# A four-layer image kernel: mixer output and last projection merged into one centred matrix, and a gate computed as one pass of 96 output rows

## The chip, the cores and the metric

The kernel runs on one core of a Trainium2 chip. The metric is the device time of one execution in microseconds (us). Each kernel was run three times; the median is given with the lowest and the highest run.

## What is computed

The input is a batch of 8 images with 256 channels and 32 x 32 pixels, in float32. Four residual layers follow each other, `x = x + layer(group_norm(x))` with 32 groups: a softmax attention on normalised queries and keys with 8 heads of 64 channels (layer 0), a 3 x 3 convolution with scaled sign weights (layer 1), a 3 x 3 convolution (layer 2), and a mixer (layer 3). The mixer is where the change lies. Cut to what matters:

```python
xs  = tokens(group_norm(x))                  # 1024 tokens x 256 channels
xm  = mamba(layernorm(xs)) + skip * layernorm(xs)    # 4 branches of 64 channels
Q   = conv1d(conv1d(xm, qdw_w, qdw_b, groups=4, pad=1), qpw_w, qpw_b)   # 256 -> 4 -> 4
xg  = sigmoid(Q) * xm                        # one gate per branch and token
R   = conv1d(depthwise3(xg), rpw_w) + xg
xm2 = conv1d(depthwise3(concat(xs, R)), fpw_w) + xs
x_local  = depthwise3(xm2, lc_w, lc_b)
x_global = mha(xm2)                          # ... attention output o, then
                                             # o @ attn_outw.T + attn_outb
x_out = concat(x_local, x_global) @ fc_w.T + fc_b
x_out = gelu(layernorm(x_out))               # over the 256 channels of a token
xi    = depthwise_conv3x3(instance_norm(x_out))
out   = layernorm(xi) @ proj_w.T + proj_b
```

The layernorm after `fc_w` subtracts, for each token, the mean over the 256 channels, and divides by the root of the mean square of what is left. All biases of this layer's setup are zero except `m_dtb`; the kernel treats them as given.

## The kernel before

**Layout.** Channels lie on the 128 partitions, in two tiles of 128 channels, and the 1024 tokens lie along the free axis. Everything is float32. A product with 256 input and 256 output channels is 8 matmuls of 128 x 128 weights and 512 columns: two output tiles, two input tiles, two halves of the tokens. In a trace every such float32 matmul appears as two records.

**Recording and order.** Operations of TensorE, VectorE and ScalarE go through the helper class `Paced` (L91 to L112), so the profile shows nearly all of them at line L101 and they are told apart by tile names. A scheduler places the instructions of each engine; each engine then works through its own queue in order and waits at an instruction whose inputs or buffers are not there. All DMAs are issued by SP, also in order. `urgent()` (L124) gives the small operations of a statistic a higher place in the schedule.

**Pools.** Large intermediates come from a pool of 12 work tiles, matmul results from two PSUM tiles of 1024 columns (`big`), one of 512 (`acc`) and two of 512 for the scans (`da`). Streamed weights come through `chunk` (L149 to L157), from six slots.

**Images in a pipeline.** For image b, `front_attention` (L576, layer 0) and `front_convs` (L750, layers 1 and 2) come first; then `scan_layers` (L1000), the selective scans of the mixer, which use VectorE, GpSimd (POOL), ScalarE and a little of TensorE; then `back_layers` (L1151), `back_out` (L1237) and `back_end` (L1263), the rest of the mixer. The main loop runs, for each b, the scans of image b beside the dense work of other images: the back layers of image b-1 and the front of image b+1. `interleave` (L1335) does this with costs: each `yield` of the dense stream gives a cost (about the TensorE time in us), and whenever the sum of costs passes a due time the next piece of the scans is recorded and the due time grows by PACE (1.8 for the first image, 2.95 for the middle six, 1.6 for the last). What is left of the scans when the dense stream ends is recorded behind it; with the given costs nothing is left. In a middle step the dense costs add up to 459.4 and the scans' due times to 433.6. After the loop, the back layers of the last image run alone.

**The order inside a middle step.** `dense()` (L1369) runs `back_layers` of image b-1 to its end, with its mixer attention (`mixer_attention`, L1044); then four pieces of the next image's front, which are the products for the values V (`islice(front, 4)`); then the first two pieces of `back_out`, which are the product with `attn_outw` (tile name `aout`, result `glob`); then one more piece of the front, the first pair's Q and K; then the rest of `back_out`, the product of the concatenated `local` and `glob` with `fc_w`; then the front's attention; then the two convolutions of the front with `back_end` laid between.

**The places that the change touches.**

- `back_layers`, L1156 to L1172: the gate. For both token halves, two channel tiles and three taps, `qdw[:, j, k]` (128 x 4) is multiplied with the tokens shifted by one tap: 12 matmuls with 4 output rows. One ScalarE pass adds the bias and gives `q4` (4 x 1024). Four matmuls with `qpr` (4 x 128) spread it over the channels, and tanh and a multiplication follow.
- `mixer_attention`, `take` and `finish` (L1092, L1119, L1136): the attention output `o` is multiplied by the inverse of the sums and the value bias is added, one VectorE pass each. The inverse comes through `invert` (L472): a DMA to DRAM and back, a reciprocal, and a DMA that spreads it (`rs<-inv`).
- `back_out`, L1237: `project_both` (L390) with `aout`, 8 matmuls; a ScalarE pass for each half of `glob`; `project_both` with `fcw`, 16 matmuls; a ScalarE pass for each half of the result `xo`, which goes to DRAM.
- `back_end`, L1263: `xo` is loaded again; `layer_norm` (L293) multiplies it with `mean_w` (4 matmuls), subtracts (VectorE, tile names `xo<-xo,big`), squares (ScalarE, `ln_sq`), and sums the squares by matmuls into `acc`.

Beside them matter `group_stats` (L256), whose chain of small matmuls and small VectorE operations must end before a convolution can begin (`im` is its normalised input), and `scan_steps` (L885).

## Time and profile before

| | |
|---|---|
| median of 3 runs | 6621.78 us (6604.92 to 6635.64) |
| the profiled execution | 6632.25 us |
| span in its profile | 6630.4 us |
| mean granted TensorE clock | 0.892 |
| TensorE matmul busy | 5708.6 us, 86% of the span |
| VectorE, ScalarE, GpSimd busy | 59%, 41%, 40% |
| DMA queue of SP | 467.90 MB, 25.4% of 16 engines |

A group row of the profile gives line, engine, operation, output and input tile with their shapes, the count, the busy time, the mean of one in ns, and the idle time of the engine just ahead of them with what ended it. For matmuls, `128*4` means 128 rows (contraction) by 4 columns of weights (output rows). In a timeline, `[8.44 <-DVE o L101]` means that the engine stood idle for 8.44 us and that a VectorE instruction that writes `o` ended it. The windows view gives the busy time of each engine in a stretch of the span.

In the trace the gate of the eight images starts at 1007.0, 1780.7, 2562.4, 3340.5, 4118.8, 4900.6, 5668.5 and 6298.3 us. These marks divide the span: up to 1007 us the front of the first two images and the first scans; six middle stages of 768 to 782 us; a stage of 630 us with the last scans; and the last image's back layers, alone, 332 us.

### The profile page before, as it was taken

The page shows a single profiled execution, that of the slowest core. Times are in us where ns is not written, and L with a number is a line of the kernel's source. Part 1 is how long each engine was busy: PE and PEld are TensorE (multiplying, and loading weights), DVE is VectorE, ACT ScalarE, POOL GpSimd, SP SyncE. Part 2 cuts the span into 40 slices and gives each one's busy share as a digit, 9 for nine tenths or more (in the row PEclk, how much of TensorE's full clock was granted, in tenths as well). Part 3 has the DMA queues.
Part 4 walks back from the last instruction along what each step waited for, and adds up shares of the span by engine and source line. Part 5 has one row for each costly group of instructions (what it writes and reads, how often), then busy time and mean ns, then how long its engine had stood idle before and what let it go on. Part 6 is the DMA issues. An engine that isn't in the chain of part 4 may idle for free.

```text
span 6630.4 us, 52730 instructions
## 1 busy us (share of the span) xinstructions
PE 5708.6 (86%) x17602; PEld 1926.6 (29%) x17602; DVE 3903.6 (59%) x4613; ACT 2687.2 (41%) x3225; POOL 2684.8 (40%) x1295
## 2 busy tenths in 40 slices
PE   8887689897998979998899989999799988978596
PEld 2331133222422234222332223222342223311222
DVE  4248745577465775567655675557755676455522
ACT  4134424553254532544245432555235442344242
POOL 0016662634355251642526334462526426176300
PEclk9988888998998989899999989899899999867697
DMA  1022332322233122331223222241213212233200
GB/s 41 27 60 79 77 90 73 101 60 65 74 97 91 48 69 76 88 83 52 76 78 92 70 64 80 72 110 45 79 59 105 79 53 80 65 94 89 58 21 26
DMA packets 217969, 471.36 MB, mean 71 GB/s; under 512 B 60244, under 2 KB 103636, under 8 KB 215640
## 3 DMA queue, kind: packets, MB, share of 16 engines
q1 hardware_dynamic: 217688, 467.90, 25.4%
q8 instruction: 141, 2.31, 0.1%
q14 instruction: 140, 1.15, 0.1%
HBM read 395.36 MB, written 63.96 MB: 69 GB/s over the span
## 4 chain that ended last, share of the span: by engine, by line
PE 53%; DVE 25%; DMA 6%; issue 6%; ACT 5%; POOL 4%; SPq 1%; POOLq 0%; DVEq 0%; ACTq 0%
PE big L101 34%; PE acc L101 12%; DVE hs L101 5%; PE da L101 4%; DVE p L101 3%; PE y L101 2%; DVE u L101 2%; DVE dw L101 2%; POOL hs L963 2%; POOL hs L931 2%; DVE t L101 1%; DVE dt L101 1%; DMA du_m<-a 1%; DVE st L101 1%; ACT p L101 1%
## 5 line engine op out<-in xcount | busy, mean ns | idle before, releaser
L931 POOL TENSOR_TENSOR hs<-du,bc 128x1024 f32<-128x1024 f32 x512 | 1319.8, 2594 | 1912.6 <-DMA du<-du_m 767.4
L963 POOL TENSOR_TENSOR hs<-hs,bc 128x1024 f32<-128x1024 f32 x512 | 1278.8, 2498 | 693.2 <-DVE hs L101 480.4
L101 ACT ACTIVATE p<-big 128x1024 f32<-128x1024 f32 x1024 | 1036.1, 1019 | 769.3 <-PE big L101 764.8
L101 PE MATMUL acc<-p,v 128*64 128x512 f32 x4096 | 1189.7, 653 | 2.6 <-ACT o L101 2.6
L101 PE MATMUL big<-im,w 128*128 128x512 f32 x2304 | 1073.7, 622 | 120.9 <-ACT im L101 102.6
L101 ACT ACTIVATE da<-dt,a_neg 128x512 f32<-128x512 f32 x1024 | 688.7, 687 | 791.3 <-DVE hs L101 484.3
L101 DVE TENSOR_TENSOR p<-p 128x1024 f32<-128x1024 f32 x448 | 717.0, 1600 | 273.7 <-ACT p L101 183.9
L101 DVE TENSOR_TENSOR_SCAN hs<-da,carry,hs 128x512 f32<-128x512 f32 x512 | 628.2, 1268 | 382.8 <-POOL hs L931 301.2
L101 DVE TENSOR_TENSOR_SCAN hs<-da,hs 128x512 f32<-128x512 f32 x512 | 600.0, 1207 | 256.8 <-ACT da L101 166.3
L101 PE MATMUL big<-q,k 64*128 64x512 f32 x2048 | 602.5, 657 | 76.7 <-ACT p L101 47.8
L101 PE MATMUL big<-qk,qk 32*128 32x512 f32 x2048 | 658.2, 687 | 9.2 <-ACT p L101 6.5
L101 PEld LDWEIGHTS big<-im,w 128*128 128x128 f32 x2304 | 445.4, 198 | 752.0 <-issue 613.8
L101 PE MATMUL y<-hs,sel 128*32 128x512 f32 x2048 | 410.9, 676 | 210.9 <-POOL hs L963 180.8
L962 POOL COPY carry<-hs 128x2 f32<-128x2 f32 x256 | 97.5, 381 | 947.6 <-DVE hs L101 928.2
L101 PEld LDWEIGHTS acc<-p,v 128*64 128x64 f32 x4096 | 217.6, 140 | 843.2 <-issue 759.8
L101 PEld LDWEIGHTS big<-qk,qk 32*128 32x128 f32 x2048 | 173.8, 195 | 487.2 <-issue 269.2
L101 PEld LDWEIGHTS big<-q,k 64*128 64x128 f32 x2048 | 161.2, 188 | 503.0 <-issue 247.4
L101 PE MATMUL big<-o,w 128*128 128x512 f32 x384 | 196.2, 664 | 92.6 <-DVE o L101 92.6
L101 PE MATMUL big<-xn,w 128*128 128x512 f32 x512 | 232.4, 608 | 5.6 <-ACT p L101 5.6
L101 DVE SCALAR_TENSOR_TENSOR dw<-xo,vec,dw 128x961 f32<-128x961 f32 (+1 forms) x128 | 194.1, 1550 | 29.3 <-ACT dw L101 29.1
L101 DVE SCALAR_TENSOR_TENSOR u<-raw,vec,u 128x1024 f32<-128x1024 f32 x96 | 153.9, 1603 | 87.2 <-ACT u L101 86.7
L101 DVE SCALAR_TENSOR_TENSOR xt<-big,vec,xt 128x1024 f32<-128x1024 f32 x48 | 61.4, 1279 | 236.2 <-PE big L101 236.2
(191 smaller groups left out, 5231.1 us busy)
## 6 DMA issues: line engine op xcount, KB each, us to landing
bc<-bc SPq DMA_DIRECT2D x1024, 128.0 KB
dt<-dt_m SPq DMA_DIRECT2D x512, 128.0 KB
du<-du_m SPq DMA_DIRECT2D x512, 128.0 KB
w<-in_wc SPq DMA_DIRECT2D x192, 192.0 KB
rs<-inv SPq DMA_DIRECT2D x64, 256.0 KB
dt_m<-dt SPq DMA_DIRECT2D x64, 256.0 KB
du_m<-a SPq DMA_DIRECT2D x64, 256.0 KB
xt<-in_x SPq DMA_DIRECT2D x8, 1024.0 KB
```

Source lines behind the costliest of these rows:

```text
L101: made = issue(*args, **kwargs)
L931: nc.gpsimd.tensor_mul(u["hs"], u["du"], both_groups(u["bc"][:, 0]))
L962: nc.gpsimd.tensor_copy(carry[:, u["q"], g : g + 2], hs[:, :, HALF - 1])
L963: nc.gpsimd.tensor_mul(hs, hs, both_groups(u["bc"][:, 1]))
```

## The change

1. **Once, near the start of the program** (`merge_weights`): `attn_outw` is multiplied on TensorE with the half of `fc_w` that takes the attention output, and the biases are carried through, so that one matrix maps `o` to `x_out`. From every column of the resulting 512 x 256 matrix, and from its bias, the mean over the 256 outputs is subtracted, so that `x_out` has mean zero over the channels by construction. The matrix is stored to DRAM (`fc_w`) and streamed from there like the other weights. This stream of instructions is placed behind the ninth piece of the first image's `front_attention`.
2. **`back_out`**: the product with `aout` and the passes that make `glob` are gone; `fcw` takes `local` and `o`. In `dense()`, the Q and K of the next image's first pair now come ahead of the whole of `back_out`.
3. **`mixer_attention`**: the value bias is no longer added to `o` (it is in the merged bias).
4. **`layer_norm`** has a switch `centred`; with it the mean matmuls and the subtraction are left out. It is used for the first layer norm of `back_end`.
5. **The gate**: one product of all three taps at once: the weights of tap k stand in columns 32k to 32k+3 of 96, so 4 matmuls give 96 rows. Three ScalarE passes of 32 rows copy them with a shift of one token to the right, none, and one to the left; the two tokens at the ends are set to zero. The following matmuls contract over 96 rows instead of 4. The cost given to the planner here is 4 instead of 10.

With both, the dense costs of a middle step add up to 446.6 instead of 459.4 (of the step of the last scans 240.5 instead of 253.4); the scans' due times are as before.

The core of the diff:

```diff
@@ chunk
-        src = I[name]
+        src = fc_w if name == "fcw" else I[name]
@@ setup
-    qpw = wp.tile([NB, NB], F32, name="qpw")
-    nc.sync.dma_start(out=qpw, in_=I["qpw"])
+    qpw = wp.tile([96, NB], F32, name="qpw")
+    nc.gpsimd.memset(qpw, 0.0)
+    for k in range(3):
+        nc.sync.dma_start(out=qpw[k * 32 : k * 32 + NB], in_=I["qpw"])
...
-    qdw = wp.tile([P, 2, 3, NB], F32, name="qdw")
+    qdw = wp.tile([P, 2, 3, 32], F32, name="qdw")
@@ layer_norm
         for tok, psum in parts:
+            if centred:
+                for t in range(2):
+                    scalar.activation(sq[t][:, tok], ts[t][:, tok], AF.Square)
+                continue
@@ mixer_attention
-                    def finish(r):
-                        vector.tensor_mul(ot, ot, r)
-                        vector.tensor_scalar_add(ot, ot, col("ain_b", 4 + t))
-                    return invert(sums[t], 4, 32, finish)
+                    return invert(
+                        sums[t], 4, 32, lambda r: vector.tensor_mul(ot, ot, r)
+                    )
@@ back_layers
         for h in range(2):
-            n = 0
             for j in range(2):
-                for k in range(3):
-                    tensor.matmul(
-                        ps[0:NB, HALVES[h]],
-                        qdw[:, j, k],
-                        xm[j][:, k + h * HALF : k + (h + 1) * HALF],
-                        start=n == 0,
-                        stop=n == 5,
-                    )
-                    n += 1
-        scalar.activation(q4[0:NB, 0:N], ps[0:NB], AF.Identity, bias=qdwb)
-        yield 10
+                tensor.matmul(
+                    ps[0:96, HALVES[h]],
+                    qdw[:, j].rearrange("p k n -> p (k n)"),
+                    inner(xm[j])[:, HALVES[h]],
+                    start=j == 0,
+                    stop=j == 1,
+                )
+
+        vector.memset(q4[0:32, 0:1], 0.0)
+        vector.memset(q4[64:96, N - 1 : N], 0.0)
+        for k, to, at in (
+            (0, slice(1, N), slice(0, N - 1)),
+            (1, slice(0, N), slice(0, N)),
+            (2, slice(0, N - 1), slice(1, N)),
+        ):
+            rows = slice(k * 32, k * 32 + 32)
+            scalar.activation(
+                q4[rows, to], ps[rows, at], AF.Identity, bias=qdwb[rows]
+            )
+        yield 4
@@ new function, called once
+    def merge_weights():
+        a, f = work("aw")[:, 0:N], work("fw")[:, 0:N]
...
+        for m in range(2):
+            nc.sync.dma_start(out=to_c[:, m], in_=I["aout"][m])
+            nc.sync.dma_start(out=f[:, m], in_=I["fcw"][m])
+        nc.sync.dma_start(out=to_j, in_=I["aout_t"])
...
+        column(lambda m, k: to_c[:, m, k], lambda k: col("ain_b", 4 + k), "aout_b", ab)
+        column(lambda m, k: f[:, m, 2 + k], lambda k: ab[:, k : k + 1], "fc_b", fc_b)
+        ps = big_tile()
+        for j in range(2):
+            for k in range(2):
+                tensor.matmul(
+                    ps[:, j * HALF : j * HALF + C].rearrange("p (m n) -> p m n", m=2),
+                    to_j[:, k, j * P : (j + 1) * P],
+                    f[:, :, 2 + k],
+                    start=k == 0,
+                    stop=k == 1,
+                )
...
+        for k in range(4):
+            vector.tensor_scalar(
+                f[:, :, k], f[:, :, k], mean[:, k, 0:1], None, ALU.subtract
+            )
...
+        for m in range(2):
+            nc.sync.dma_start(out=fc_w[m], in_=f[:, m])
+        yield 0
@@ back_out
-        glob = [work("glob0"), work("glob1")]
-        def evac_glob(m, ps):
-            scalar.activation(
-                glob[m][:, 0:N], ps, AF.Identity, bias=col("aout_b", m)
-            )
-        yield from project_both("aout", o, evac_glob)
...
-            scalar.activation(xo, ps, AF.Identity, bias=col("fc_b", m))
+            scalar.activation(xo, ps, AF.Identity, bias=fc_b[:, m : m + 1])
...
-        yield from project_both("fcw", local + glob, evac_fc)
+        srcs = [t[:, 0:N] for t in local + o]
+        yield from project_both("fcw", srcs, evac_fc)
@@ main loop
-    drain(front_attention(image_of(0), imgs[0]), front_convs(imgs[0]))
+    drain(
+        amid(front_attention(image_of(0), imgs[0]), merge_weights(), (8,)),
+        front_convs(imgs[0]),
+    )
...
             yield from islice(front, 4)
-            ending = back_out(last)
-            yield from islice(ending, 2)
             yield next(front)
-            yield from ending
+            yield from back_out(last)
```

## The prediction, as it was put on record

> **What bounds the kernel now.** I read the page's first part and its chain of waits, then the rows by shape, then the timeline of one middle stage.
>
> ```profile
> PE 5708.6 (86%) x17602; PEld 1926.6 (29%) x17602; DVE 3903.6 (59%) x4613; ACT 2687.2 (41%) x3225; POOL 2684.8 (40%) x1295
> ...
> PE 53%; DVE 25%; DMA 6%; issue 6%; ACT 5%; POOL 4%; SPq 1%; POOLq 0%; DVEq 0%; ACTq 0%
> ```
>
> PE leads in busy time and in the chain, so what leaves PE's queue, or shortens a wait in it, counts. The price of a matmul comes from its rows by shape:
>
> ```profile
> L101 PE MATMUL big<-xn,qdw 128*4 128x512 f32 x192 | 83.7, 592 | 0.0
> ...
> L101 PE MATMUL big<-xo,mean_w 128*128 128x512 f32 x64 | 35.6, 701 | 11.7 <-DMA xo<-xo_d 11.7
> ...
> L101 ACT ACTIVATE q<-big,qdwb 4x1024 f32<-4x1024 f32 x8 | 8.8, 1104 | 257.9 <-PE big L101 257.9
> ```
>
> Records overlap, so the mean is not the price. The 24 records of a gate run 10.46 us in the timeline, the last one 0.59: (10.46 - 0.59) / 23 = 0.43 us per record, 0.86 us per matmul at full clock. With 4 output rows it costs what one with 128 does.
>
> Two places in the stage from 2562 us, the first at the product with `aout`:
>
> ```profile
> 2862.34 3.70 PE L101 MATMUL big<-o,w 128*128 128x512 f32 x8
> ...
> 2873.67 0.75 DVE L101 TENSOR_SCALAR o<-o,vec 128x1024 f32<-128x1024 f32 x1
> ...
> 2874.48 6.66 PE L101 MATMUL big<-o,w 128*128 128x512 f32 x8 [8.44 <-DVE o L101]
> ```
>
> PE does half of `aout`, stands for 8.44 us for the second tile of `o`, and then runs at half speed (6.66 us for what took 3.70). Behind it in the queue stand the next image's Q and K (7.03 us) and the `local` half of the last projection (7.13 us), which need nothing from `o`. The second place is the start of the first convolution:
>
> ```profile
> 3106.13 1.17 DVE L101 TENSOR_TENSOR xo<-xo,big 128x1024 f32<-128x1024 f32 x1
> ...
> 3113.04 0.58 PE L101 MATMUL acc<-d,gmat 128*128 128x2 f32 x2 [4.79 <-DVE d L101]
> ...
> 3140.25 9.92 PE L101 MATMUL big<-im,w 128*128 128x512 f32 x19 [10.42 <-ACT im L101]
> ```
>
> The convolution waits for a chain of small DVE operations, and the layer norm's two subtractions (1.17 and 1.21 us) and scans lie between them. How far DVE can be relieved there the windows view tells:
>
> ```profile
> 3102.00:3140.00 38.00, 17.29 (x62) 9.90 (x60) 33.58 (x51) 10.86 (x12) 15.81 (x6) 0.68 0.12 35
> ...
> 3180.00:3220.00 40.00, 32.71 (x72) 11.46 (x72) 40.00 (x32) 7.61 (x12) 31.61 (x14) 0.83 0.18 53
> ```
>
> The third number after the length is PE, then PEld, DVE, ACT, POOL: DVE is nearly full in both, so PE can't be had there for nothing.
>
> [...] 6.66 against 3.70 us behind the 8.44 us wait. So a wait that goes takes a slow stretch with it. [...] the trace has 86 ns for 4 columns and about 195 for 128, both beside a running matmul, so 96 columns are hidden. [...] the trace has 1.10 for 4 rows and 1.11 for 128 (`glob`). A pass of 32 rows is thus taken at 1.10 us.
>
> **The change, part by part.** I also read the order in which the built program's instructions stand.
>
> *Counts.* Per image 8 gate matmuls, 8 of `aout` and 4 of the mean go: 20 x 0.86 = 17.2 us of PE at full clock, 137 us for eight images. ACT is even: two `glob` passes go, two gate passes come. DVE loses two subtractions and two bias passes (1.66 us each by their row) and gains two sets of one column (0.06 each). SP loses two loads per image.
>
> *A, `aout` and the order around it, middle stages.* In the new order Q and K (7.0), one group of scan sums (1.1), the `local` matmuls (7.1) and the products of a scan branch (1.9) stand ahead of the first matmul that needs `o`: 17.1 us from the end of V. The second tile of `o` came 12.1 us after that point (2874.4 - 2862.3), and comes 0.75 us sooner without its bias pass. The wait goes, with 5 us to spare. Gained: 8.44 + (6.66 - 3.70) + 16 records of `aout` (6.9) = 18.3 us; in the other five middle stages the wait is 8 to 11 us. The next attention needs the new Q and K, which have 14 us of matmuls over them as before. I take 17. Bounds: 8, where the DMA chain of `o` is held up on SP by 10 us more (its `rs<-inv` stands behind the scans' loads); 21 = the whole stretch between the two attentions (67 us mean) less the 46 us that the new order's matmuls add up to.
>
> *B, the gate.* 8 matmuls fewer: 6.9 us. The statistics that stand behind it have their data at 3343.4 and PE would be free at 3340.5 + 3.4 = 3344.0, so that chain starts at once. Two more passes (2.2 us) lie on ACT; they end at about 3347.4, when the `xn` pass behind them gets its input anyway (3348). `qpr` waits for them, but the gate's tanh stood behind `xn` before too. I take 6, bounds 5 and 7. For the last image nothing covers the passes: 6.9 - 2.2 = 4.7.
>
> *C, the centred projection.* 4 matmuls fewer, but they ran beside the statistics of `xt` and hid behind these; on the path are the two subtractions, 2.4 us. In the new order no scan stands between the difference `d` and the shift, which could take most of the 10.4 us wait for `im`, but DVE must do those scans just behind, where it was full. I take 4; bounds 2.4 and 12.
>
> *Middle stages:* 17 + 6 + 4 = 27, six of them: 162 us.
>
> *Stage of the last scans (5668 to 6298).* The second tile of `o` comes at 6161.5; from there to the mean matmuls `aout`, `local` (with a 7.6 us wait for its weights) and `glob` took 38.8 us, of which some 15 (one product, its pass, the DMA) stay: 23 us sooner, with C 27. But the scans run until about 6265 in this stage, at POOL's pace, and the new order has their last products behind the second layer norm. I take 16 for this and 6 for B: 22, bounds 10 and 34.
>
> *Last image, alone.* `local` runs during the wait for `o` (10.1 us before), then 16 records of `o` partly at half clock, two passes, the DMA: squares at about 6523 and their sums at 6524 against 6546.6: 22. With B 27, bounds 22 and 30.
>
> *Merging, once.* Its loads follow Q and K weights that SP had issued by 39.9 us, so the data lie there when PE arrives at about 53 us. On PE 14 small matmuls, some 4 us, and three returns to DVE with about 1 us each, with two `big` tiles shared with the attention that PE is bound by (2.07 us a unit): 10 us, bounds 5 and 20. Queued behind it are the scores on PE, hence the exponentials on ACT; the stores hold SP's queue, behind which only later weights stand. Two more small loads at the start: 0.6 us, in the bounds.
>
> *Sum:* 162 + 22 + 27 - 10 = 201 us of the profiled execution's 6632 (3.03%): 6431. It stands 10 us above the median, so on the median 6621.8 x 0.9697 = 6421.
>
> **Rivals.** *The scans take the gain back* (still faster). The costs of a middle step fall by 12.9, the scans' due times don't, so the scans lie denser and 4.4 pieces later, into the stretch where DVE was full. For it: 40.00 of 40 us; 18.6 us per stage in which PE waits for POOL's products. Against: in the stage's last 80 us DVE is busy for 27.6 and POOL for 30.3. If a middle stage keeps only the 10 us of B and C: 60 + 10 + 22 - 15 = 77, on the median 6545.
>
> *More than counted.* The wait for `im` goes for the most part (12 for C), and A comes to 20: 39 x 6 + 28 + 28 - 8 = 282, 6340.
>
> *Slower: the gate waits for the scans at each stage's end.* Before, 20 matmuls (17 us) stood between the last scan product and the gate; in the new order it is 14 (12 us). If POOL and DVE run behind PE by more than these 12 us plus the 27 gained, 39 us, the stage ends with the scans, and each us more is lost six times; at 52 us late it is 6 x 13 - 39 = 39 us slower, 6661. For it: pieces bunched at the end. Against: POOL's 336 busy us of 778, and its idle time in that end.
>
> *The change does nothing to speak of*, because these stretches were covered: the waits are PE's own, so I give it little: 6615.
>
> **Chances.** Forecast (6370 to 6490) 0.60; scans take it back (6490 to 6590) 0.20; more (below 6370) 0.12; same 0.04; slower 0.04. The bounds together give (8 + 5 + 2.4) x 6 + 10 + 22 - 20 = 104 (6518) at one end, and (21 + 7 + 12) x 6 + 34 + 30 - 5 = 299 (6323) at the other. With the rivals 6345 to 6545 leaves no more than 2 in 10 out. About 0.5% is what a measurement can tell here: faster 0.92, same 0.04, slower 0.04.
>
> **What would show it.** A: no wait for `o` ahead of the last projection, and less than 55 us between the two attentions. B: 8 records of `qdw` in a run of 3.6 us, the next statistics 6 us sooner. C: the wait for `im` at the first convolution below 10 us. Merging: the first attention about 10 us longer. Middle stages of about 750 us instead of 778. Wrong: a wait for `o` or `xn` that moves to another instruction, or longer waits of PE for POOL's `hs` in the convolutions.

## The result: slower, and where the time lies in the profile after

| | before | after |
|---|---|---|
| median of 4 runs, us | 6617.29 (6604.92 to 6635.64) | 6783.12 (6771.58 to 6802.24) |
| ratio, 95% interval | | 1.025 (1.021 to 1.029) |
| the profiled execution, us | 6632.25 | 6773.59 |
| span, us | 6630.4 | 6771.8 |
| mean granted TensorE clock | 0.892 | 0.859 |

The change costs 166 us on the median; 201 us less was forecast. From the page of the kernel after (the helper's line is now L102) come its engines and the row of the score products of the mixer attention; the last line is the same row of the kernel before:

```profile
PE 5753.1 (85%) x17310; PEld 1933.1 (29%) x17310; DVE 3974.1 (59%) x4610; ACT 2690.7 (40%) x3225; POOL 2685.5 (40%) x1297
...
L102 PE MATMUL big<-qk,qk 32*128 32x512 f32 x2048 | 734.6, 769 | 31.5 <-ACT p L102 29.2
...
L101 PE MATMUL big<-qk,qk 32*128 32x512 f32 x2048 | 658.2, 687 | 9.2 <-ACT p L101 6.5
```

PE has 292 records fewer and is busy 44.5 us longer. The work went, and what is left runs slower: a score record of the mixer attention takes 769 ns on the mean, where it took 687. DVE's 70 us more are no new work either (it has three instructions fewer); the traces do not say why its instructions took longer.

The start of each image's gate divides both spans alike. The part ahead of the first gate grew by 8.5 us (1007.0 to 1015.5), the six middle stages by 164 (4661.5 to 4825.6), the stage of the last scans shrank by 4 (629.8 to 625.4), the last image alone by 27 (332.2 to 305.2). So the loss lies in the middle stages. One of them, the third stretch between gates, by the windows view (length, then busy time and count of PE, PEld, DVE, ACT, POOL, then the granted clock). Before:

```profile
2562.40:2649.80 87.40, 81.29 (x221) 36.70 (x220) 58.60 (x100) 33.90 (x37) 0.00 (x0) 0.90 0.22 70
2649.80:2839.20 189.40, 173.20 (x621) 40.93 (x620) 102.57 (x98) 115.67 (x141) 127.31 (x66) 0.90 0.35 93
2839.20:2905.60 66.40, 55.80 (x148) 21.01 (x148) 37.59 (x42) 22.43 (x30) 37.84 (x16) 0.92 0.34 94
2905.60:3082.40 176.80, 170.15 (x626) 45.39 (x628) 132.58 (x139) 98.89 (x120) 51.75 (x26) 0.99 0.20 56
3082.40:3140.20 57.80, 34.60 (x108) 16.62 (x104) 41.66 (x59) 13.22 (x17) 15.81 (x6) 0.79 0.17 51
3140.20:3340.50 200.30, 178.46 (x484) 75.57 (x484) 119.05 (x138) 51.08 (x63) 103.47 (x47) 0.92 0.29 80
```

After:

```profile
2612.20:2694.80 82.60, 72.21 (x205) 35.97 (x203) 58.69 (x96) 36.08 (x38) 0.00 (x0) 0.90 0.18 59
2694.80:2914.30 219.50, 202.81 (x623) 45.65 (x622) 92.19 (x93) 114.71 (x139) 120.44 (x65) 0.77 0.31 84
2914.30:2965.20 50.90, 45.03 (x124) 17.20 (x122) 38.41 (x41) 19.75 (x26) 31.83 (x13) 0.97 0.25 73
2965.20:3155.60 190.40, 172.21 (x626) 46.10 (x624) 139.69 (x137) 94.93 (x115) 57.28 (x24) 0.96 0.20 53
3155.60:3205.10 49.50, 33.88 (x105) 16.59 (x105) 30.33 (x53) 14.45 (x18) 17.86 (x10) 0.77 0.33 92
3205.10:3417.80 212.70, 183.85 (x493) 77.72 (x494) 139.57 (x154) 55.88 (x69) 107.93 (x52) 0.89 0.27 80
```

The rows are: gate to mixer attention, mixer attention, V and last projection, front attention, from there to the first convolution, convolutions. The three rows in which work was taken out became shorter, by 4.8, 15.5 and 8.3 us. The three in which no work was changed became longer, by 30.1, 13.6 and 12.4. The largest is the mixer attention: the same work, 0.77 of the clock instead of 0.90. The clock records there have 99 us at half clock after, 37.5 before.

How such a stretch begins is seen in PE's timeline of the kernel after, at the attention's begin:

```profile
2694.83 1.13 PE L102 MATMUL big<-qk,qk 32*128 32x512 f32 x4
2696.28 1.99 PE L102 MATMUL big<-qk,qk 32*128 32x512 f32 x8 [0.32 <-DVE qk L102]
2698.20 1.08 PE L102 MATMUL acc<-p,v 128*64 128x512 f32 x4
2703.11 2.08 PE L102 MATMUL big<-qk,qk 32*128 32x512 f32 x4 [3.83 <-ACT p L102]
2705.11 1.98 PE L102 MATMUL acc<-p,v 128*64 128x512 f32 x4
...
2716.85 1.98 PE L102 MATMUL acc<-p,v 128*64 128x512 f32 x4
2718.76 1.92 PE L102 MATMUL y<-hs,sel 128*32 128x512 f32 x4
2720.61 1.47 PE L102 MATMUL big<-qk,qk 32*128 32x512 f32 x4
2722.01 1.08 PE L102 MATMUL acc<-p,v 128*64 128x512 f32 x4
```

After a wait of 3.83 us each unit takes twice its time (2.08 and 1.98 instead of 1.13 and 1.08) for four units, although PE has no gap, until a group of scan products (`y<-hs,sel`) has passed. The clock records have 20.5 us at half clock here, of which PE works 18.3 us without a gap:

```profile
2700.90:2721.40 20.50, 18.29 (x38) 3.89 (x40) 2.34 (x2) 8.35 (x10) 7.17 (x4) 0.50 0.39 96
```

The wait comes from ScalarE, and ScalarE's from a scan:

```profile
2696.01 1.02 ACT L102 ACTIVATE p<-big 128x1024 f32<-128x1024 f32 x1 [9.98 <-PE big L102]
2700.82 1.30 ACT L102 ACTIVATE da<-dt,a_neg 128x512 f32<-128x512 f32 x2 [3.79 <-DMA dt<-dt_m]
2702.05 1.91 ACT L102 ACTIVATE p<-big 128x1024 f32<-128x1024 f32 x2
```

The first exponential of the new scan stands in ScalarE's queue behind the attention's first `p` and waits there for its data; the attention's next `p` wait behind it. Nothing in the diff touches these instructions. What the change did to them is the planner's cost: 4 instead of 10 for the gate puts every scan piece (10 - 4) / 2.95 = 2 places later in the recorded order, and the two pieces of `aout` that went put those behind them 6.88 / 2.95 = 2.3 places later still.

**Theories.** *Phase*: where the scan pieces fall among the dense work decides, and the change moved them to a worse place. *Order*: the new place of Q and K, with weights that come late. *Work*: with less PE work the scans' engines bound the stage.

### The profile page after: what moved, and what is told of

Read it like the earlier page. It is cut to its first block, busy times and chain, and to the rows that moved or that the text cites. A ratio compares the mean times of both kernels' runs of the same rounds, so it can differ in the third digit from the quotient of the medians.

```text
span 6771.8 us, 52155 instructions
## 1 busy us (share of the span) xinstructions
PE 5753.1 (85%) x17310; PEld 1933.1 (29%) x17310; DVE 3974.1 (59%) x4610; ACT 2690.7 (40%) x3225; POOL 2685.5 (40%) x1297
## 4 chain that ended last, share of the span: by engine, by line
PE 59%; DVE 23%; issue 5%; ACT 5%; DMA 4%; POOL 2%; SPq 1%; DVEq 0%; POOLq 0%; ACTq 0%
PE big L102 37%; PE acc L102 14%; PE da L102 6%; DVE p L102 6%; DVE hs L102 5%; PE y L102 3%; DVE dw L102 2%; DVE t L102 2%; POOL hs L942 1%; DVE u L102 1%; DVE dt L102 1%; POOL hs L974 1%; DMA dt<-dt_m 1%; DVE st L102 1%; ACT p L102 1%
## 5 line engine op out<-in xcount | busy, mean ns | idle before, releaser
L102 ACT ACTIVATE p<-big 128x1024 f32<-128x1024 f32 x1024 | 1038.6, 1020 | 1000.8 <-PE big L102 977.4
L102 PE MATMUL acc<-p,v 128*64 128x512 f32 x4096 | 1261.0, 688 | 29.5 <-ACT o L102 27.0
L102 PE MATMUL big<-im,w 128*128 128x512 f32 x2304 | 1072.6, 622 | 54.2 <-ACT im L102 36.7
L102 ACT ACTIVATE da<-dt,a_neg 128x512 f32<-128x512 f32 x1024 | 689.8, 687 | 888.9 <-DVE hs L102 673.0
L102 DVE TENSOR_TENSOR p<-p 128x1024 f32<-128x1024 f32 x448 | 793.0, 1770 | 296.9 <-ACT p L102 169.7
L102 DVE TENSOR_TENSOR_SCAN hs<-da,carry,hs 128x512 f32<-128x512 f32 x512 | 625.4, 1265 | 332.2 <-POOL hs L942 216.7
L102 DVE TENSOR_TENSOR_SCAN hs<-da,hs 128x512 f32<-128x512 f32 x512 | 598.9, 1207 | 375.9 <-POOL hs L942 221.5
L102 PE MATMUL big<-qk,qk 32*128 32x512 f32 x2048 | 734.6, 769 | 31.5 <-ACT p L102 29.2
L102 PE MATMUL big<-q,k 64*128 64x512 f32 x2048 | 604.6, 661 | 68.5 <-ACT p L102 40.9
L102 PEld LDWEIGHTS big<-im,w 128*128 128x128 f32 x2304 | 448.5, 199 | 696.1 <-issue 615.6
L102 PE MATMUL y<-hs,sel 128*32 128x512 f32 x2048 | 409.3, 700 | 204.4 <-POOL hs L974 204.3
L102 PEld LDWEIGHTS acc<-p,v 128*64 128x64 f32 x4096 | 226.6, 146 | 930.0 <-issue 810.1
L102 PEld LDWEIGHTS big<-qk,qk 32*128 32x128 f32 x2048 | 191.2, 216 | 566.6 <-issue 260.6
L102 PE MATMUL big<-xn,w 128*128 128x512 f32 x512 | 255.7, 657 | 60.0 <-DMA w<-in_wqk 29.0
L102 PEld LDWEIGHTS big<-q,k 64*128 64x128 f32 x2048 | 163.1, 191 | 496.2 <-issue 260.2
L102 DVE SCALAR_TENSOR_TENSOR dw<-xo,vec,dw 128x961 f32<-128x961 f32 (+1 forms) x128 | 227.4, 1806 | 29.8 <-ACT dw L102 29.1
L102 PE MATMUL da<-xn,w_minw 64*128 64x512 f32 x256 | 150.7, 705 | 81.5 <-DVE hs L102 80.9
L102 PE MATMUL big<-o,w 128*128 128x512 f32 x384 | 189.6, 646 | 11.4 <-DVE o L102 11.4
L102 DVE SCALAR_TENSOR_TENSOR u<-raw,vec,u 128x1024 f32<-128x1024 f32 x96 | 136.5, 1422 | 106.4 <-ACT u L102 105.2
```

The source lines that it names most:

```text
L102: made = issue(*args, **kwargs)
```

## Experiments

Each kernel is compared with the kernel before on the same chip; the medians of before were 6619 to 6647 us. Where kernels that ran on different chips are set against each other, the fair measure is the distance of each from before on its own chip. It matters for `after_aout_costs` and the two kernels with holds, beside which before took 6647 us; beside all others it took 6617 to 6627.

All edits are to the changed kernel unless said.

**1. Costs alone.** The old costs in the changed kernel, and the new costs in the kernel before.

```diff
@@ changed kernel: after_old_costs
-        yield 4
+        yield 10
@@
+            yield 3.44
+            yield 3.44
             yield next(front)
             yield from back_out(last)
@@ kernel before: before_new_costs
-        yield 10
+        yield 4
-            yield from islice(ending, 2)
+            for _ in islice(ending, 2):
+                yield 0
```

The two empty pieces also stand in the step of the last scans, here and in `after_aout_costs`.

> The changed kernel, with the planner's costs of the kernel before: 10 for the gate, and two empty pieces of 3.44 where the product with aout was. All of the changed work stays; only where the scan pieces lie among the dense work goes back to its old place. Theory (phase): the middle stages got longer because the scan pieces fall 2 to 4 places later against the attentions, PE then waits there for POOL, DVE and DMA and falls into half clock; so this kernel should come near the forecast, 6400 to 6520 us, with half clock in a mixer attention back from 99 to about 40 us. Rival (order): the new place of Q and K ahead of the projection, and the weights that come late for it, cost the time; then it stays at 6700 to 6790. Rival (work): less dense PE work leaves the scans' engines as the bound; then too it stays above 6650.

Measured: 6366.05 us, ratio to before 0.961 (0.959 to 0.963).

> The kernel before, all of its work as it was, with the planner's costs of the changed kernel: 4 instead of 10 for the gate, 0 for the two pieces of the product with aout. Phase theory: the same displacement of the scan pieces by itself makes it slower, by 20 to 45 us in each of six middle stages, so 6740 to 6890 us. Rivals (order, work): no change, 6600 to 6640.

Measured: 6927.52 us, 1.047 (1.044 to 1.050).

The old costs undo the loss of 166 us and bring 254 us more; the new costs, put into the kernel before, cost 307 us with not one instruction changed. Phase holds; order and work fall as causes that act by themselves. The new order has a small part together with the new costs: in the kernel after, PE waits 4.7 to 5.1 us for weights of Q and K in each of the six middle stages, 29.0 us in all. With the old costs, and with the new costs in the kernel before, no such wait is in the profile. Both went further than expected: 6366 us where 6400 to 6520 was said, and 6928 where 6740 to 6890 was. The page of the changed kernel with old costs, and ScalarE at the same place as above:

```profile
PE 5495.9 (86%) x17310; PEld 1886.1 (30%) x17310; DVE 3850.2 (60%) x4610; ACT 2689.3 (42%) x3225; POOL 2682.2 (42%) x1297
```

```profile
2573.05 1.28 ACT L102 ACT_TABLE_LOAD   x1 [17.59 <-DMA dt<-dt_m]
2574.34 1.30 ACT L102 ACTIVATE da<-dt,a_neg 128x512 f32<-128x512 f32 x2
2575.58 1.00 ACT L102 ACTIVATE p<-big 128x1024 f32<-128x1024 f32 x1
```

Here the scan's exponential stands ahead of the first `p`, and its data has come when the attention begins. Both kernels have 17310 PE records. Of the 399 us between the spans (6771.8 - 6372.9), 257 are these records running slower (5753.1 - 5495.9), and 142 are PE standing idle.

**2. The gate alone**, in the kernel before, with the new cost and with the old one (`before_new_gate`, `before_new_gate_c10`):

```diff
@@ kernel before, with the changed setup of qpw, qdwb, qdw and qpr
-                for k in range(3):
-                    tensor.matmul(
-                        ps[0:NB, HALVES[h]],
-                        qdw[:, j, k],
...
+                tensor.matmul(
+                    ps[0:96, HALVES[h]],
+                    qdw[:, j].rearrange("p k n -> p (k n)"),
...
@@ before_new_gate
+        yield 4
@@ before_new_gate_c10
+        yield 10
```

> The kernel before with the gate of 96 rows alone, cost 4 as in the changed kernel. By itself it saves 6 us a stage. Phase theory: the cost of 10 that became 4 moves the scans by two places, about half of the whole displacement, so it loses more than it gains: 6640 to 6720 us. Rivals (order, work of the merged matrix): it gains its 6 us in each of seven stages and 5 in the last, 6570 us.

Measured: 6919.46 us, 1.045 (1.042 to 1.048).

> The kernel before with the gate of 96 rows alone and the old cost 10, so that the scan pieces keep their places. Theory (phase): the work saved shows, by the forecast's own step B 6 us in each of seven stages and 4.7 in the last, 47 us: 6573 us, against 6919 us of the same gate with cost 4. Rival (the new gate itself does harm, through its three ScalarE passes or its 96 columns of weights): 6700 or more.

Measured: 6568.33 us, 0.992 (0.989 to 0.995).

The gate itself gives 59 us (6627.42 - 6568.33); with the cost of 4 the same kernel is 299 us slower than before (6919.46 - 6619.98), so this cost takes about 359 us. I had put the first at 6640 to 6720, in proportion to the displacement: the loss is not in proportion.

**3. A map of the costs.** Single edits of the planner's numbers:

```diff
@@ after_gate10; after_gatem2 has -2
-        yield 4
+        yield 10
@@ after_aout_costs
+            yield 3.44
+            yield 3.44
             yield next(front)
@@ after_pace287
-    PACE = [1.8] + [2.95] * (batch - 2) + [1.6]
+    PACE = [1.8] + [2.87] * (batch - 2) + [1.6]
```

> The changed kernel with cost 10 for the gate and no empty pieces for aout: the scans lie as in the kernel before up to the end of the mixer attention, and two places later behind it. Theory (phase): the mixer attention is as in the kernel with all old costs (179 us, 24 us half clock), and the front attention and the convolutions stay as slow as in the changed kernel (10 and 12 us per middle stage over it): 6366 + 6 x 22 = 6500 us. If the gate's cost is all that matters: 6370 to 6400. If aout's: 6700 or more.

> The changed kernel with cost -2 for the gate: the scan pieces come two places later still than in the changed kernel. If lateness itself costs the time (the scans' work pushed against the stage's end), it is slower than the changed kernel by about as much as that is slower than the one with cost 10, 6900 us or more. If single collisions decide (which wait falls where in the attention), the sign is open: 6550 to 6900.

> The changed kernel with cost 4 for the gate and the two empty pieces of 3.44 where the product with aout was: the other corner beside gate 4 without (6783), gate 10 without (6506) and gate 10 with (6366). If the two displacements add (the gate's works in the mixer attention, aout's behind it): 6783 - 140 = 6643 us. If single collisions decide, no sum holds: the scan pieces behind the mixer attention then lie two places late, as in no other run, 6550 to 6850.

> The changed kernel with PACE 2.87 instead of 2.95 in the middle steps, so that the scans' due times shrink in the ratio in which the dense costs did (446.6 to 459.4). The scans end as early against the dense work as before, but within the step each piece lies elsewhere than in the kernel before. Phase theory in its simple form (the scans are too late as a whole): 6450 to 6600 us. If instead single collisions decide, each pace gives another set of them, and the time can be anywhere from 6500 to 6800. Rival (order): 6750 to 6800.

| gate's cost | without the empty pieces | with them (6.88) |
|---|---|---|
| 10 | 6506.37 | 6366.05 |
| 4 | 6783.12 (the change) | 6749.55 |
| -2 | 6860.19 | |
| 4, PACE 2.87 | 6678.31 | |

Their ratios to before: 0.982 (0.979 to 0.985) for 10, 1.016 (1.012 to 1.019) for 4 with the pieces, 1.035 (1.033 to 1.038) for -2, 1.009 (1.007 to 1.011) for the pace. Measured from before on each one's chip, the four corners of the table are 121 and 254 us faster (cost 10, without and with the pieces) and 166 and 103 us slower (cost 4). So the gate's cost is worth 287 us without the pieces and 357 with them, the pieces 133 or 63: the displacements do not add, which I had taken as the first possibility (6643). The cost of 10 alone came out as expected (6500). To put the density right by PACE, at other places, wins back 105 of the 417 us, so that the theory in its simple form (6450 to 6600) is missed.

Each displacement of the gate's cost made the kernel slower, but not in proportion: 287 us for the first two places, 67 for the next two. With -2 the middle mixer attentions are shorter than after (206 to 208 us against 209 to 220), but the stretch behind them is some 70 us instead of 51; some 25 us of it is one wait of PE, in five of the six stages for weights of Q and K. So lateness is no smooth price, and what a place costs depends on the waits that fall there. That single collisions decide is a reading of these profiles; no run took one of them away.

**4. Why half clock lasts.** The clock records change in steps of 3.41 us. I sorted these windows in eleven traces with 32-row scores (all but `after_aout_costs` and the holds), taking the half-clock windows in which PE never stood still. Where 32-row products held four tenths of the time or more, 2 of 932 were followed by full clock; where they held one tenth to under four, 173 of 236; where they held less, 1059 of 1420. The mixer attention alone, half scores by time, is of the first sort. Products of 64 rows, such as the scores of the front attention, do not behave so: where they held four tenths or more, 139 of 197 windows were followed by full clock. Nor do the 32-row scores end full clock by themselves: in the kernel after, the last image's mixer attention, alone (6531.3 to 6663.4 us), ran at a clock of 1.00 throughout, with PE busy for 131.8 of 132.1 us. In the timeline above half clock begins in a wait of 3.83 us; the 32-row scores seem to keep it. Two edits test this. The first contracts over all 128 rows (the scores are then sums of four heads, which changes the output):

```diff
@@ after_rows128
-                "q": [qk[t][r, 0:N] for r in rows],
-                "k": [qk[2 + t][r, 0:N] for r in rows],
+                "q": [qk[t][:, 0:N] for r in rows],
+                "k": [qk[2 + t][:, 0:N] for r in rows],
```

> The changed kernel, order and costs untouched; only the score products of the mixer attention contract over all 128 rows of q and k (four heads together) instead of the 32 rows of one head, so that the scores are sums of four heads and the output differs from the reference. Number, size and place of the instructions are the same. The windows of 3.41 us in the clock records of six traces suggest a condition for the return from half clock: full-busy half-clock windows in which the 32-row products hold 4 tenths of the time or more were followed by full clock in 2 of 570 cases. Theory (rows): the attention alone cannot lead PE back to full clock, and the stretches of 82 to 99 us of half clock per mixer attention are as long as they are because of this; with 128 rows they end after one or two windows, 20 to 45 us of half clock stay, 20 to 35 us are won per middle stage, and the time is 6540 to 6650 us. Rival (waits alone): the waits set the length of the half-clock stretches; nothing changes, 6760 to 6800 us.

Measured: 6912.32 us, 1.044 (1.041 to 1.047). The mixer attention of the third stretch, windows view as above, and its first 12 score records:

```profile
2739.40:2972.30 232.90, 219.91 (x623) 63.82 (x621) 92.67 (x93) 116.00 (x139) 120.47 (x65) 0.96 0.30 82
```

```profile
2739.42 5.31 PE L102 MATMUL big<-qk,qk 128*128 128x512 f32 x12
```

The clock is 0.96, half clock fell from 99 to 20.5 us, with PE idle for 13.0 us against 16.7 (length less busy time): the clock did what the theory says. The time did not, because the edit had a second effect: 12 records take 5.31 us, where the changed kernel's first 12 take 1.13 + 1.99, that is 0.44 us a record against 0.26. In the trace of the changed kernel the 32-row score records start in pairs, 0.007 us apart (the first at 2694.832 and 2694.839 us); by the times, the products of a pair no longer ran at once with 128 rows. My expectation missed that, and this run alone settles nothing about time.

The second edit keeps the result and takes 64 rows, as the front attention does; there the four score records of a unit take 1.13 us (kernel before, at 2908.86 us), as the four with 32 rows do above. A pair is two heads 64 rows apart, and the key rows of each one's neighbour are zero (the second copy of the keys lies in the convolutions' input tiles, idle at that time, whose edges are set to zero again later).

```diff
@@ after_masked64
+                for e, k in enumerate((qk[t], odd[t])):
+                    vector.tensor_scalar(
+                        k[:, 0:N], ps, col("ain_b", t), heads_of[:, e : e + 1],
+                        ALU.add, ALU.mult,
+                    )
@@
-                "q": [qk[t][r, 0:N] for r in rows],
-                "k": [qk[2 + t][r, 0:N] for r in rows],
-                "v": [v_of(i), v_of(i + 1)],
+                "q": [qk[t][r, 0:N] for r in two],
+                "k": [(odd if i % 2 else qk)[2 + t][r, 0:N] for r in two],
+                "v": [v_of(i), v_of(i + 2)],
```

> The changed kernel, costs and order untouched; in the mixer attention two heads that are 64 rows apart form a pair, and each score product contracts over 64 rows, with the key rows of the other head set to zero, so that the result is the reference's. [...] Added: two VectorE passes of 1.28 us ahead of each mixer attention, and eight small memsets. Theory (rows): half clock in a mixer attention falls from 82 to 99 us to 15 to 40 us with about the same waits, worth 25 to 38 us per middle stage and up to 85 in the stage of the last scans, less 3 per stage: 6440 to 6570 us. Rival (waits alone): 6780 to 6810.

Measured: 6545.73 us, 0.988 (0.985 to 0.992). The same stretch, and PE behind the same early wait:

```profile
2648.50:2831.80 183.30, 167.01 (x623) 40.38 (x624) 96.89 (x98) 114.63 (x139) 122.00 (x65) 0.95 0.37 101
```

```profile
2656.85 1.13 PE L102 MATMUL big<-qk,qk 64*128 64x512 f32 x4 [2.47 <-ACT p L102]
2657.91 1.91 PE L102 MATMUL acc<-p,v 128*64 128x512 f32 x4
2659.75 1.95 PE L102 MATMUL big<-qk,qk 64*128 64x512 f32 x4
2661.63 1.08 PE L102 MATMUL acc<-p,v 128*64 128x512 f32 x4
```

The wait is still there, 1.4 us shorter; the slow stretch behind it is one window of 3.4 us instead of 20.5, with no scan product in it. In the whole attention, three half-clock stretches of 3.4 to 6.8 us stand where five of 13.7 to 30.7 us stood. It is 183.3 us long instead of 219.5, with PE idle for 16.3 us against 16.7. The changed costs are as they were, so 237 us (6783.12 - 6545.73) come from this edit. It changed more than the number of rows: other heads form a pair, and half of the key rows are zero. No run separates these; that 64-row windows, such as those of the front attention with neither, were followed by full clock too (139 of 197) speaks for the rows.

The same with the old costs of experiment 1:

> The same masked 64-row scores in the changed kernel with the old costs. A middle mixer attention has 24 us of half clock there, so little is to be won in the middle stages (about what the two passes cost); the stage of the last scans has 314 us of half clock, of which 100 may go, 50 us of time: 6310 to 6360 us. If the rows are what makes the phase costly, the distance between this and the run with the new costs shrinks from 417 us to under 200.

Measured: 6317.52 us, 0.954 (0.950 to 0.957), the fastest of all. The distance between new and old costs is 228 us with 64 rows, 417 with 32. Under 200 was expected if the rows are what makes the phase costly; the edit takes 189 us of the 417 away, and the larger part is left. With 64 rows it lies in the front attention (190 against 180 us in a middle stage), the convolutions (216 against 201) and the mixer attention (183 to 186 against 176 to 180).

**5. The price of one wait.** `after_late_exp` records the first unit's exponentials one piece later, to take the wait of 3.83 us away:

```diff
+            if n == 0:
+                stages[1:3] = (0, None), (0, decays)
```

> The changed kernel; of each image's scans only the first unit's two exponentials (da from dt) are recorded one piece later, so that on ScalarE they stand behind more of the attention's exponentials and no longer hold these up while dt is on its way. Theory (a wait of a few us starts a long half-clock stretch): PE's wait of 3.8 us, 8 us after the attention's begin, goes, and with it the first stretch of 20 us at half clock, 10 to 14 us per middle stage: 6690 to 6730 us. Rival (the next wait takes its place, since the scan product behind it comes later): 6760 to 6800.

Measured: 6788.98 us, 1.025 (1.022 to 1.029). The profile has the wait as before (3.86 us, at 8.3 us of the attention): the scheduler put the exponentials at the same place in ScalarE's queue. The edit did not do what it was for, and nothing follows.

Two further runs put waits in instead, into the kernels with the old costs:

```diff
             scalar.activation(p, s, AF.Exp)
+            for _ in range(6 * (u["n"] in held_up)):
+                scalar.activation(p, p, AF.Copy)
@@ held_up
+ (13, 29, 45)
```

> The changed kernel with the old costs (6366 us), and at three of the 64 units of each mixer attention (13, 29 and 45) six copies of the probabilities onto themselves on ScalarE, 1.02 us each, which hold up the exponentials behind them by some 6 us and PE by 4 to 5 us: 24 holds in all. Theory (rows): behind each wait PE stays at half clock until the next scan products of 128 rows come, some 10 to 20 us, which costs 5 to 10 us more: 9 to 15 us per hold, 6580 to 6730 us. Rival (a wait costs its own length and one window): 5 to 7 us per hold, 6480 to 6530 us.

Measured: 6486.55 us, 0.976 (0.973 to 0.980).

> The same holds in the kernel with the old costs and masked 64-row scores (6318 us). Theory (rows): the clock comes back after one or two windows of 3.41 us, so a hold costs its 4 to 5 us and 2 to 3 us of half clock: 6460 to 6510 us, clearly less per hold than in the kernel with 32 rows. Rival (rows do not matter for the price of a wait): the same rise in both kernels.

Measured: 6459.15 us, 0.972 (0.969 to 0.975).

Measured from before on each one's chip, the 24 holds cost 94 us with 32 rows (254 us faster without them, 160 with them) and 114 us with 64 rows (301 and 187), 4 to 5 us each; the plain differences of 120 and 142 us contain a slower chip. The theory's expectation of 9 to 15 us per hold with 32 rows, and of clearly less with 64, is missed; its rival, that the rows do not matter for the price of a wait, fits. The edit held PE up less than planned: at the holds of the third stretch it waited only 0.9, 1.8 and 3.6 us with 32 rows. Half clock in that attention rose by 17 us in both kernels, from 24 to 41 with 32 rows and from 17 to 34 with 64. So not every wait in this attention begins a long slow stretch. What makes the difference between these waits and those of the kernel after is not shown.

**6. The centring alone.** `old_costs_uncentred` is the changed kernel with the old costs and with the mean products and subtractions of the first layer norm back (they subtract zero).

```diff
-        yield from layer_norm(xo, sq, WHOLE, acc_tile, affine("lgn_w", "lgn_b", AF.Gelu), True)
+        yield from layer_norm(xo, sq, WHOLE, acc_tile, affine("lgn_w", "lgn_b", AF.Gelu))
```

> The changed kernel with the old costs and the mean products and subtractions of the first layer norm put back (they subtract a mean that is zero). This is step C by itself, at the old places of the scans: by the forecast 4 us per middle stage (bounds 2.4 to 12) and a few in the last: 6390 us; if C is what made the gain larger than forecast, 6420 to 6440.

Measured: 6438.28 us, 0.973 (0.969 to 0.976). The centring is worth 72 us, in the range set for the case that C made the gain larger than forecast.

## Why the prediction was wrong

**The step that failed** is the one that the sum lacks. The forecast saw the costs fall by 12.9 and the scans come "4.4 pieces later", and put its price in the sum at nothing. The rival "The scans take the gain back" priced it, at no more than the gain of A: a middle stage keeps B and C; the chances' lower end kept 8 us of A besides. It looked for the harm where DVE was full, in the convolutions. Two of those 4.4 pieces come from the gate and act from the stage's begin on, on the mixer attention, which the forecast did not look at. There was no reason to end the bounds at a gain: pieces in new places can cost more than the change saves, and here did. The displacement costs 417 us in the changed kernel (6783.12 - 6366.05) and 307 us in the kernel before, against the 201 us that the change was to save. A middle stage has 27 us more on the mean (164 / 6) where 27 less were forecast.

**The slower rival** had the wrong place. It let the gate wait for the scans at the stage's end. The gate waits for nothing there (its 8 records begin straight behind the last convolution product); the time is lost inside, in three stretches whose work the diff does not touch.

**"A wait that goes takes a slow stretch with it"** was right and one-sided. The forecast had read one such stretch, 6.66 us of work behind a wait of 8.44 us. In the kernel after, PE worked without a gap for 18.3 us at half clock behind a wait of 3.83 us, in the mixer attention with 32-row scores; with 64-row scores the half-clock stretches of that attention were one or two windows long (3.4 to 6.8 us, `after_masked64`). A wait that comes can bring a stretch much longer than the forecast would have charged for it, though the holds of experiment 5 did not.

**The steps that were counted**, read at the scans' old places:

| step | forecast, us | measured, us |
|---|---|---|
| B, gate | 47 (36 + 6 + 5) | 59 (6627.42 - 6568.33) |
| C, centring | 24 in the middle stages | 72 (6438.28 - 6366.05), all stages |
| A and the merging, with the rest | 130 | 123, what is left (254 - 59 - 72) |
| sum | 201 | 254 (6619.98 - 6366.05) |

The last row but one is a difference of kernels, which takes the steps to add. The windows view of the changed kernel with old costs, in the third stretch, shows where the 254 us come from. It is 37.7 us shorter than before (740.4 against 778.1): 5.7 from the gate to the mixer attention, 14.1 between the attentions, 10.8 from there to the convolution, and 10.7 in the mixer attention, which nobody forecast, less 3.2 in the front attention and 0.4 in the convolutions. So the three named places give 30.6 us where 27 was said, and part of what exceeds the forecast is luck: the unchanged mixer attention ran better.

- A: the mechanism right, the size 14.1 us where 17 was said. In the kernel after, the stretch between the attentions is 50.9 us (under 55 was said), and no wait for `o` stands there.
- B: right in the middle stages, 5.7 us where 6 was said; of the 59 us that the gate alone gave, 23 lie in the mixer attentions of the middle stages, whose work is the same. In the kernel after, the 8 records take 3.60 us as said, with weight loads of 163 ns for 96 columns (before: 86 for 4) and copies of `q` of 1.10 us for 32 rows, and the mixer attention begins 4.8 us sooner after the gate, a little under the lower bound of 5; PE waits there for the copies of `q`:

```profile
2612.22 3.60 PE L102 MATMUL big<-xn,qdw 128*96 128x512 f32 x8
...
2619.25 3.78 PE L102 MATMUL big<-q,qpr 96*128 96x512 f32 x4 [2.28 <-ACT q L102]
```

- C: the mechanism right, the size too small. The wait for `im` fell from 10.42 to 1.36 us, in the kernel after too, and the stretch ahead of the convolution became 10.8 us shorter where 4 was said, near the upper bound of 12. The reason for the low value, that DVE must do the displaced scans just behind, did not hold at the old places: there the convolutions are as long as before (200.7 against 200.3 us).

```profile
3205.06 1.22 PE L102 MATMUL big<-im,w 128*128 128x512 f32 x1 [1.36 <-ACT im L102]
```

- Merging: 8.5 us where 10 was said, but loosely: ahead of the first gate the traces without merging took 1007.0 to 1011.4 us, those with it 1011.3 to 1016.9. Last image: 27 where 27 was said. Stage of the last scans: 4 where 22 was said; with the old costs it is 27 (629.8 to 602.5).
- A slip of reading: in the two windows lines of the forecast, the first number after the length is PE and the third is DVE. The text names the third as PE; its conclusion, DVE nearly full, is what the lines show.

**What stays open.** Which collisions make the front attention and the convolutions 10 to 15 us longer with the new costs is not settled. PE's waits of the kernel after (total, times, longest) point to the scans (`hs`), the depthwise convolution of `back_end` (`dw`) and the sums of probabilities (`p`), all on DVE, and to the weights of Q and K:

```profile
PE da L102 <- DVE hs L102: 103.8, 32, 7.8
PE big L102 <- DVE dw L102: 88.5, 9, 29.0
...
PE big L102 <- DVE p L102: 71.8, 28, 8.4
...
PE big L102 <- DMA w<-in_wqk: 29.0, 6, 5.1
```

With the old costs the first three are 65.7, 47.3 and 27.5 us, and the last is absent. DVE itself is busy for 124 us less there with the same 4610 instructions (3850.2 against 3974.1); what slows it was not looked for. That is a reading of two profiles; no run took these waits away. Nor was the first long stretch traced to one wait by an edit, since experiment 5 did not move it.

## What to carry to other kernels

In a kernel whose streams are interleaved by written costs, the costs are part of the schedule: when an edit makes a piece cheaper, change the work first with the old cost, measure, and tune the cost by itself. Here that order gives 0.961, both at once 1.025. For the forecast: an edit of a cost has no sign from the diff, so its bound is open on both sides, and the first thing to read is what each engine's queue holds at the displaced places (here ScalarE's, where the scan's first exponential waited 3.79 us for its data with the attention's `p` behind it).

## What the runs showed of the hardware that was not expected

- Once at half clock, PE seldom came back to full clock while 32-row products held four tenths of the time or more (2 of 932 windows), though it was never idle. It came back in 173 of 236 windows in which they held one tenth to under four, and in 139 of 197 in which 64-row products held four tenths or more. With 64-row scores in the mixer attention, whose added key rows were zero, half clock there fell from 99 to 17 us. A rule for all kernels does not follow.
- The same 32-row scores did not bring half clock about where PE did not wait: 132.1 us at a clock of 1.00.
- The score records with 32 rows start in pairs, 0.007 us apart: 12 records took 3.1 us (1.13 + 1.99), against 5.31 us with 128 rows each (`after_rows128`).
